# Moving work between VectorE and ScalarE around a branch: second half of batch 0's layernorm sums, sums of the weights, and the order of a few small steps

## The chip, the cores and the metric

The kernel runs on one core of a Trainium2 chip. The metric is the time of one execution on the device in microseconds (us), as the median of a few runs. A core has five engines that work side by side, each through its own list of instructions in order: TensorE (in the profile PE for matmuls, PEld for weight loads), VectorE (DVE), ScalarE (ACT), GpSimd (POOL) and SyncE (SP), which here only issues transfers. They wait for one another through semaphores. TensorE writes its results to PSUM, in banks of 128 x 512 numbers, and VectorE or ScalarE must take them from there before a bank can be used again.

## What is computed

Two graph layers over 32 batches of 512 x 512, all in float32. Each begins with a layernorm over the last axis and a maximum with 0. Layer 0 aggregates with `adj` and multiplies with a weight; layer 1 is attention with eight heads and a mask.

```python
# layer 0
h = jnp.maximum(_layernorm(x, axis=-1), 0.0)
x = x + einsum('bnd,do->bno', einsum('nm,bmd->bnd', adj, h), weight) + bias
# layer 1
h = jnp.maximum(_layernorm(x, axis=-1), 0.0)
q, k, v = h @ Wq + bq, h @ Wk + bk, h @ Wv + bv          # 8 heads of 64
scores = einsum('bqhd,bkhd->bhqk', q, k) / sqrt(64) + (1.0 - adj) * -1e9
x = x + einsum('bhqk,bkhd->bqhd', softmax(scores), v) @ Wo + bo
```

The mask subtracts (1 - adj) x 1e9. Where a row of `adj` has a largest entry that is ahead of the next by enough, the softmax puts the whole weight on that one place, and attention is a copy of the row of h that stands there. The kernel proves this from bounds at its start, and then computes layer 1 as h @ (Wv Wo) for the rows that are pointed at, and gathers the results. A general path exists for other inputs; it doesn't run here.

## The kernel before

A 512 x 512 matrix lies in SBUF as a tile of 128 partitions by four chunks of 512. Most products are made by `product()` (line 445): it splits each matrix in 2 x 2 blocks of 256 and forms the result from seven block products instead of eight, with sums of blocks prepared on VectorE. `sum_a` (line 324) makes the four sums of the left matrix, `sum_b` (line 336) those of the right, each one VectorE instruction over 128 x 512. The seven pieces come in the order p1, p5, u2, c11, c22, c12, c21. Three PSUM banks are added up over several pieces: p1, u2, c22 and c21 share one, so u2 can't begin before p1's value was taken out. A piece is taken by a `take`: in the product that forms yT (`take_new`) ScalarE copies p1, p5, u2 and c21 (line 490) and VectorE adds c11, c22 and c12 (line 488); in the product of layer 0 (`take_onto`) VectorE adds all seven onto x (line 508).

**Ahead of the branch** (lines 88 to 308) the order of the instructions is written out by hand. Wv and Wo are folded into wvo (`fold`, line 142, seven block products as above); adj is turned over on TensorE (`transposed`); batch 0 is normalised (`norms[0]`, `norms[1]`, two chunks each). `peaks(c)` (line 155) finds the eight largest entries of a chunk of adj's rows and marks where the first stands. `both` adds the four marks, TensorE counts them by columns (line 261), and `used` (line 279) says which rows of h are pointed at. TensorE counts these (line 264), VectorE decides (`decide`, line 243), TensorE spreads the decision (line 269), and `flag` (line 292) goes to every engine, which branch on it (lines 310 to 317). Beside this, layer 0's aggregate of batch 0 (line 270) runs on TensorE in four groups d = 0 to 3 of four products.

**Behind the branch** `single_path` (line 405) loops over the batches. For each, `todo` holds 21 lists of small steps, filled with `put(batch, step, function)`. They are handed out in three rows of seven: steps 0 to 6 go with the pieces of layer 0 of batch b, 7 to 13 with those of the aggregate of batch b + 1, and 14 to 20 with those of layer 1 of batch b - 1. In front of a piece's take, the functions of its step are issued (lines 477 to 480), so a step stands in each engine's list ahead of that take. For b = 0 the first row is `layer0_rows` (line 573) with only four steps, steps 4 to 6 are added to step 3, and the third row has no products: its steps are issued at once.

A layernorm comes in two kinds with the same interface. `Norm` (line 348) takes the sums of a row on VectorE (BATCH_NORM_STATS2, line 359, and an aggregate, line 360). `NormAct` (line 381) takes them on ScalarE, with two activations that add up along the row (line 389), each followed by a read of the accumulator. In both, `power()` makes 1 / sqrt(variance + eps) on GpSimd (lines 366 and 398), `offset()` makes the bias on VectorE, and `relu()` applies all on ScalarE (line 377). `halves` are the two halves of batch b's second layernorm, of layer 1, each over two of the four chunks.

Two queues matter for what follows. GpSimd scatters the rows of h to DRAM (`put_h`, line 582) with four indirect transfers in steps 9 and 11; SP loads them back in another order (`get_h`, line 597, step 16) and loads the next x.

Of the kernel before, what the change touches and what calls it, by code (L numbers as in the profile page):

```python
# [25 lines left out]
def gnn_two_layers(ctx: ExitStack, tc: tile.TileContext, x, adj, w0, b0, wq, bq, wk, bk, wv, bv, wo, bo, out):  # L26
# [15 lines left out]
    nc = tc.nc  # L42
# [10 lines left out]
    adjT, yT, w0_s, sel, wvo = big("adjT"), big("yT"), big("w0_s"), big("sel"), big("wvo")  # L53
# [18 lines left out]
    with ExitStack() as tmp, tc.manual_schedule():  # L72
# [82 lines left out]
        def peaks(c):  # L155
            nc.vector.max(top[:, c, :], adj_s[:, c, :])  # L156
            nc.vector.tensor_scalar(sel[:, c, :], adj_s[:, c, :], top[:, c, 0:1], None, op0=ALU.is_equal)  # L157
# [15 lines left out]
        u, v, w = (bank(i) for i in (0, 1, 2))  # L173
# [27 lines left out]
        flips = transposed(adj_s, adjT)  # L201
        next(flips)
        fold(u, wvT_t[:, 2], wo_t[:, 2], False)
        peaks(1)
        norms[1].offset()
        nc.vector.tensor_add(blk(wvo, 1, 1), u, blk(wvo, 1, 1))
        next(flips)
        next(flips)
        fold(v, wvT_t[:, 3], wo_blk(1, 1), False)
# [46 lines left out]
        for d in range(DC):  # L256
            ps = bank((2, 1, 0, 2)[d]).rearrange("p a n -> p (a n)")
            for m in range(C):
                if d == 1 and m == 2:
                    for i in range(C):  # L260
                        nc.tensor.matmul(few[:, 0, i:i + 1], both[:, i * P:(i + 1) * P], ones[:, 0:1],
                                         start=True, stop=True)
                if d == 2 and m == 1:
                    nc.tensor.matmul(many[:, 0, :], ones, used, start=True, stop=True)
                    nc.tensor.matmul(many[:, 1, :], ones, sums, start=True, stop=True)
                if d == 2 and m == 3:
                    nc.tensor.matmul(bias, ones, part, start=True, stop=True)
                if d == 3 and m == 1:
                    nc.tensor.matmul(few[0:1, 1, 0:1], sure, ones[:, 0:1], start=True, stop=True)
                nc.tensor.matmul(ps, hs[0][:, m, d * P:(d + 1) * P], adjT[:, m, :], start=(m == 0), stop=(m == C - 1))  # L270
            if d == 0:
                squares(0)
            nc.scalar.copy(yT[:, d, :], ps)
            if d == 0:
                squares(1)
                for i in range(4):
                    sum_b(nc, adjT_s, adjT, i)
            if d == 1:
                nc.vector.tensor_scalar_min(used, few[:, 0, :], 1.0)
                if B > 1:  # L280
                    norms.append(NormAct(nc, small, mhalf, xs[1], hs[1], range(C)))
                    for c in range(C):
                        norms[2].stats(c)
                for i in range(2):
                    sum_b(nc, w0_t, w0_s, i)
            if d == 2:
                decide()
                nc.vector.memset(before[:, 0:1], 0.0)
                for m in range(1, C + 1):
                    nc.vector.tensor_add(before[:, m:m + 1], before[:, m - 1:m], many[:, 0, m - 1:m])  # L290
                nc.vector.tensor_add(cvo, bias, cvo)
# [28 lines left out]
def blk(t, chunks, cols, half=256):  # L320
    return t[:, 2 * chunks:2 * chunks + 2, cols * half:(cols + 1) * half]
# [83 lines left out]
def single_path(ctx: ExitStack, tc: tile.TileContext, x, wv, bv, wo, bo, out, kept, room):  # L405
# [15 lines left out]
    nc = tc.nc  # L421
# [127 lines left out]
    def norm(src, dst, chunks, kind=Norm):  # L549
        return kind(nc, small, mhalf, src, dst, chunks)  # L550
# [152 lines left out]
    with tc.manual_schedule():  # L703
        nc.gpsimd.affine_select(out=upper, in_=ones, compare_op=ALU.is_ge, fill=0.0, base=-1,
                                pattern=[[1, P]], channel_multiplier=-1)
        for b in range(B + 1):
            todo = [[] for _ in range(21)]

            def put(batch, step, f, *args):
                if 0 <= batch < B:  # L710
                    todo[step].append(lambda: f(batch, *args))

            put(b - 2, 15 if b == B - 1 else 1, fetch if b > B - 2 else finish)
            if b < 2:
                put(b + 2, 2 * b, load_x)
            if b > 0:
                put(b + 3, 15, load_x)
            for i, step in enumerate((0, 1, 2, 3) if b != 1 else (1, 2, 3, 4)):
                put(b + 1, step, h0_sum, i)
            put(b - 2, 14 if b == B - 1 else 0, put_z, 0, 6)  # L720
            if b == B - 1:
                put(b - 2, 13, put_z, 6, S)
            for r, step in enumerate((10, 11, 12) if b in (1, B - 1) else (5, 7, 8) if b < B else ()):
                put(b - 1, step, transpose_h, r)
            for c, step in enumerate((1, 3, 9, 12) if b == 0 else (9, 10, 11, 12) if b == B - 2 else (14, 15, 17, 19)):
                put(b + 1, step, add_b0, c)
            if b < B:
                H1[b] = work.tile([P, C, D], F32, name="h1")
                halves = [norm(X[b], H1[b], [2 * i, 2 * i + 1], Norm if b > 0 else NormAct) for i in range(2)]
            put(b, 6 if b > 0 else 1, lambda b: halves[0].stats(0))  # L730
            put(b, 6 if b > 0 else 2, lambda b: halves[0].stats(1))
            put(b, 6 if b > 0 else 7, lambda b: halves[0].power())
            put(b, 7 if b > 0 else 3, lambda b: halves[1].stats(0))
            put(b, 7, lambda b: halves[0].offset())
            put(b, 10 if b == B - 1 else 8, lambda b: halves[0].relu(0, b < B - 1))
            put(b, 8 if b > 0 else 7, lambda b: halves[1].stats(1))
            put(b, 8 if b > 0 else 7, lambda b: halves[1].power())
            put(b, 10 if b == B - 1 else 9, lambda b: halves[0].relu(1, b < B - 1))
            put(b, 10 if b == B - 1 else 9, put_h, 0)
            put(b, 9, lambda b: halves[1].offset())  # L740
            put(b, 10, lambda b: halves[1].relu(0, b < B - 1))
            put(b, 10, lambda b: halves[1].relu(1, b < B - 1))
            put(b, 11, put_h, 2)
            if b < B - 1:
                put(b - 2, 12, store)
            if b < B - 1:
                put(b, 16, get_h)
            else:
                put(b, 13, get_all)
                for c in range(C):  # L750
                    put(b, 15 + c, add_cvo, c)
            for i, step in enumerate((12, 13, 13, 14) if b in (1, B - 1) else (11, 11, 12, 12) if b < B else ()):
                put(b - 1, step, hT_sum, i)
            for i, step in enumerate((13, 13, 13, 14) if b in (0, B - 2) else (14, 15, 16, 18)):
                put(b + 1, step, yT_sum, i)
            if b < B and b != B - 2:
                put(b - 1, 20, put_z, 6, S)
            ahead = []
            if b == 0:
                put(2, 1, lambda b: ahead.append(ln0(b, NormAct)))  # L760
                for c, step in enumerate((1, 1, 2, 2)):
                    put(2, step, lambda b, c: ahead[0].stats(c), c)
            else:
                put(b + 2, 8, lambda b: ahead.append(ln0(b)))
                for c, step in enumerate((9, 10, 13, 13)):
                    put(b + 2, step, lambda b, c: ahead[0].stats(c), c)
            put(b + 2, 14 if b > 0 else 11, lambda b: ahead[0].power())
            put(b + 2, 17 if b > 0 else 12, lambda b: ahead[0].offset())
            for c, step in enumerate((17, 18, 19, 20) if b > 0 else (12, 13, 14, 14)):
                put(b + 2, step, lambda b, c: ahead[0].relu(c), c)  # L770
            if b == 0:
                put(0, 1, lambda b: number_rows())
                for i in (2, 3):
                    put(0, 12, lambda b, i: sum_b(nc, w0_t, w0_s, i), i)
                    put(0, 13, lambda b, i: sum_a(nc, wvo_t, wvo, i), i)
                todo[3] += todo[4] + todo[5] + todo[6]
                run(layer0_rows(0), todo[0:4])
            if b == B - 1:
                put(b, 19, lambda b: transpose_all(0))
            if b == 1:  # L780
                tables = []
                put(1, 0, lambda b: tables.append(places()))
                put(1, 16, lambda b: look_up(tables[0]))
            if 0 < b < B:
                run(layer0(b), todo[0:7])
            elif b == B:
                run(None, todo[0:7])
            run(aggregate(b + 1) if b + 1 < B else layer1(b - 2) if b < B else None, todo[7:14])
            run(layer1(b - 1) if 0 < b < B and b != B - 2 else None, todo[14:21])
# [262 lines left out]
```

## Time and profile before

| | |
|---|---|
| median of 3 runs | 1081.98 us (1081.93 to 1082.1) |
| the profiled execution, its own time | 1081.54 us |
| its span in the trace | 1079.7 us |
| granted TensorE clock | 0.999 |
| VectorE busy / ScalarE busy / GpSimd busy | 898.7 / 376.2 / 447.1 us |
| flag written (VectorE, line 292) | at 37.05 us |
| first layer 0 product behind the branch (TensorE, line 577) | at 40.51 us |
| first aggregate product in the loop (TensorE, line 451) | at 54.77 us |
| first layer 0 product of batch 1 | at 67.98 us |

All times in the trace count from the start of the span. A line of the timeline gives the start, the busy time, the engine, the line of the kernel, the operation, what it writes and reads, and in brackets how long the engine was idle before it and what it waited for. Instructions on VectorE and ScalarE overlap a little: a sum of 128 x 512 on VectorE shows 0.68 us, and the next begins 0.60 us after its start. The waits are idle time in front of an instruction, put down to the instruction elsewhere that ended it.

### The profile page before, as it was taken

What the parts mean: (1) busy time and instruction counts of PE and PEld (TensorE: products, weight loads), DVE (VectorE), ACT (ScalarE), POOL (GpSimd) and SP (SyncE); (2) the same over time, 40 slices, a digit from 0 to 9 for tenths busy, and PEclk for the clock granted to TensorE, in tenths of its full rate; (3) what the DMA queues carried; (4) which work ended last, traced back from release to release, by engine and by line L of the source; (5) the groups of instructions that cost most, each with busy time, mean ns of one, the idle gap of its engine ahead of it and who ended that gap; (6) DMA issues with size and microseconds to landing.
All of it is one profiled execution on the core that took longest, in us unless ns stands there. A gap on an engine that the chain in (4) does not pass through costs nothing.

```text
span 1079.7 us, 16014 instructions
## 1 busy us (share of the span) xinstructions
PE 1066.3 (99%) x5448; PEld 946.2 (88%) x5448; DVE 898.7 (83%) x1837; ACT 376.2 (35%) x709; POOL 447.1 (41%) x522
## 2 busy tenths in 40 slices
PE   9999999999999999999999999999999999999996
PEld 7478989999998999988999988999998999998993
DVE  6868888888888888888888888888888888888874
ACT  4744323334422324322323432323432323432331
POOL 2024554343554343554343454443454434355413
PEclk9999999999999999999999999999999999999999
DMA  9154666657776666767666767666776666766538
GB/s 330 40 92 145 183 184 160 157 169 197 186 185 158 165 168 187 193 174 183 148 169 184 199 170 195 143 168 175 205 187 183 148 157 180 199 180 165 133 106 272
DMA packets 162700, 186.92 MB, mean 173 GB/s; under 512 B 15024, under 2 KB 102832, under 8 KB 162608
## 3 DMA queue, kind: packets, MB, share of 16 engines
q1 hardware_dynamic: 132592, 116.73, 36.8%
q0 software_dynamic: 27968, 66.61, 27.4%
q10 hardware_dynamic: 2048, 2.46, 0.7%
q8 instruction: 45, 0.74, 0.3%
q14 instruction: 47, 0.39, 0.1%
HBM read 96.28 MB, written 89.46 MB: 172 GB/s over the span
## 4 chain that ended last, share of the span: by engine, by line
PE 93%; DVE 3%; DMA 2%; issue 1%; POOL 1%; ACTq 0%; ACT 0%; POOLq 0%; DVEq 0%
PE mm L451 91%; PE mm L577 1%; DMA x<-in_L_gnn_Wv_dram 1%; PE mm L270 1%; DMA yT<-z,place 1%; DMA z<-hc 0%; POOL hs L589 0%; DVE top L156 0%; DVE part L163 0%; DVE hc L656 0%; DVE st L359 0%; POOL rstd L398 0%; DVE sel L157 0%; DVE both L223 0%; POOL yT L674 0%
## 5 line engine op out<-in xcount | busy, mean ns | idle before, releaser
L665 POOL DMA_INDIRECT x<-z,place x116 | 182.8, 1576 | 351.3 <-issue 194.3
L490 ACT COPY yT<-mm 128x512 f32<-128x512 f32 x124 | 71.9, 580 | 541.9 <-PE mm L451 538.8
L508 DVE TENSOR_TENSOR x<-mm,x 128x512 f32<-128x512 f32 x217 | 149.8, 690 | 86.9 <-PE mm L451 86.9
L377 ACT ACTIVATE h<-x,off,rstd 128x512 f32<-128x512 f32 x256 | 194.5, 807 | 39.9 <-DVE off L369 35.8
L366 POOL TENSOR_TENSOR rstd<-ve,mhalf 128x2 f32<-128x2 f32 (+1 forms) x93 | 102.5, 1102 | 200.0 <-DVE ve L365 200.0
L451 PE MATMUL mm<-w_t,sel 128*128 128x256 f32 x744 | 171.0, 379 | 1.2 <-DVE x L508 1.2
L451 PE MATMUL mm<-adjT_s,h0s 128*128 128x256 f32 x744 | 171.0, 379 | 0.9 <-ACT yT L490 0.9
L359 DVE BATCH_NORM_STATS2 st<-x 128x6 f32<-128x512 f32 x244 | 163.4, 670 | 1.1
L451 PEld LDWEIGHTS mm<-w_t,sel 128*128 128x128 f32 x744 | 141.2, 190 | 20.8 <-DVE x L508 1.6
L451 PEld LDWEIGHTS mm<-adjT_s,h0s 128*128 128x128 f32 x744 | 141.2, 190 | 20.6 <-ACT yT L490 1.5
L589 POOL DMA_INDIRECT hs<-h,dest x124 | 133.2, 1074 | 23.6 <-issue 22.4
L451 PE MATMUL mm<-w_s,yT 128*128 128x256 f32 x496 | 117.2, 379 | 0.0
L451 PE MATMUL mm<-adjT,h 128*128 128x256 f32 x496 | 117.2, 379 | 0.0
L451 PE MATMUL mm<-hTs,wvo_t 128*128 128x168 f32 x720 | 112.4, 306 | 0.0
L501 ACT ACTIVATE zs<-mm,cvo_c 128x168 f32<-128x168 f32 x240 | 83.1, 397 | 75.0 <-PE mm L451 75.0
L451 PEld LDWEIGHTS mm<-adjT,h 128*128 128x128 f32 x496 | 94.2, 190 | 13.2 <-ACT h L389 0.2
L451 PEld LDWEIGHTS mm<-hTs,wvo_t 128*128 128x128 f32 x720 | 105.5, 190 | 0.0
L451 PEld LDWEIGHTS mm<-w_s,yT 128*128 128x128 f32 x496 | 92.9, 190 | 11.3
L557 DVE TENSOR_TENSOR x<-x,b_r 128x512 f32<-128x512 f32 x124 | 84.0, 677 | 0.0
L451 PE MATMUL mm<-hT,wvo 128*128 128x168 f32 x480 | 78.2, 306 | 0.0
L451 PEld LDWEIGHTS mm<-hT,wvo 128*128 128x128 f32 x480 | 72.7, 190 | 1.6
L488 DVE TENSOR_TENSOR yT<-mm,yT 128x512 f32<-128x512 f32 x93 | 64.0, 688 | 9.4 <-PE mm L451 4.9
(181 smaller groups left out, 1313.3 us busy)
## 6 DMA issues: line engine op xcount, KB each, us to landing
out_dram<-x SPq DMA_DIRECT2D x124, 256.0 KB, 4.7
x<-in_x_dram SPq DMA_DIRECT2D x120, 256.0 KB, 4.9
hc<-hs SPq DMA_DIRECT2D x124, 176.0 KB, 3.1
z<-zr SPq DMA_DIRECT2D x120, 96.0 KB, 2.0
z<-zr SPq DMA_DIRECT2D x120, 80.0 KB, 1.9
hs<-h,dest POOLq DMA_INDIRECT x124, 6.0
x<-z,place POOLq DMA_INDIRECT x116, 5.8
adj_s<-in_adj_dram SPq DMA_DIRECT2D x2, 512.0 KB, 5.8
```

The lines of the kernel that those rows point to most:

```text
L270: nc.tensor.matmul(ps, hs[0][:, m, d * P:(d + 1) * P], adjT[:, m, :], start=(m == 0), stop=(m == C - 1))
L359: self.nc.vector.bn_stats(st, self.src[:, self.chunks[i], :])
L366: self.nc.gpsimd.tensor_tensor(self.rstd, ve, self.mhalf[:, 0:n], ALU.pow)
L377: self.nc.scalar.activation(dst, src, AF.Relu, bias=self.off[:, i:i + 1], scale=self.rstd[:, i:i + 1])
L451: nc.tensor.matmul(bank[:, m, 0:half], lhs[:, k, m * P:(m + 1) * P], rhs[:, k, :], start=(first and m == 0 and k == 0), stop=(k == 1), ski ...
L488: nc.vector.tensor_add(dst, bank, dst)
L490: nc.scalar.copy(dst, bank)
L501: nc.scalar.activation(dst[:, m, :], bank[:, m, :], AF.Identity, bias=cvo_c[:, 2 * i + m:2 * i + m + 1])
L508: nc.vector.tensor_add(dst, bank, dst)
L557: nc.vector.tensor_add(X[b][:, c, :], X[b][:, c, :], b0_r)
L589: stored = nc.gpsimd.indirect_dma_start(out=HS[b], out_offset=bass.IndirectOffsetOnAxis(ap=dest[:, i:i + 1], axis=0), in_=H1[b][:, i, :], ...
L665: nc.gpsimd.indirect_dma_start(out=X[b][:, c, :], out_offset=None, in_=Z[b], in_offset=bass.IndirectOffsetOnAxis(ap=place[:, c:c + 1], axi ...
```

## The change

Four things are moved; nothing is computed otherwise, apart from the way the sums of one half layernorm are formed.

1. Ahead of the branch, the addition of a fold product to wvo and the offset of the second half of batch 0's first layernorm stand ahead of `peaks(1)`. Before, the order was peaks, offset, addition.
2. The fourth sum of adjT stands behind `used` instead of ahead of it.
3. The second half (chunks 2 and 3) of batch 0's second layernorm is a `Norm` instead of a `NormAct`: its row sums are taken on VectorE.
4. The third and fourth sums of w0 go from step 12 to step 8, those of wvo from step 13 to step 9.

```diff
@@ -201,9 +201,9 @@
         flips = transposed(adj_s, adjT)
         next(flips)
         fold(u, wvT_t[:, 2], wo_t[:, 2], False)
+        nc.vector.tensor_add(blk(wvo, 1, 1), u, blk(wvo, 1, 1))
+        norms[1].offset()
         peaks(1)
-        norms[1].offset()
-        nc.vector.tensor_add(blk(wvo, 1, 1), u, blk(wvo, 1, 1))
         next(flips)
         next(flips)
         fold(v, wvT_t[:, 3], wo_blk(1, 1), False)
@@ -273,10 +273,11 @@
             nc.scalar.copy(yT[:, d, :], ps)
             if d == 0:
                 squares(1)
-                for i in range(4):
+                for i in range(3):
                     sum_b(nc, adjT_s, adjT, i)
             if d == 1:
                 nc.vector.tensor_scalar_min(used, few[:, 0, :], 1.0)
+                sum_b(nc, adjT_s, adjT, 3)
                 if B > 1:
                     norms.append(NormAct(nc, small, mhalf, xs[1], hs[1], range(C)))
                     for c in range(C):
@@ -726,7 +727,7 @@
             if b < B:
                 H1[b] = work.tile([P, C, D], F32, name="h1")
-                halves = [norm(X[b], H1[b], [2 * i, 2 * i + 1], Norm if b > 0 else NormAct) for i in range(2)]
+                halves = [norm(X[b], H1[b], [2 * i, 2 * i + 1], Norm if b > 0 or i == 1 else NormAct) for i in range(2)]
             put(b, 6 if b > 0 else 1, lambda b: halves[0].stats(0))
@@ -771,8 +772,8 @@
                 for i in (2, 3):
-                    put(0, 12, lambda b, i: sum_b(nc, w0_t, w0_s, i), i)
-                    put(0, 13, lambda b, i: sum_a(nc, wvo_t, wvo, i), i)
+                    put(0, 8, lambda b, i: sum_b(nc, w0_t, w0_s, i), i)
+                    put(0, 9, lambda b, i: sum_a(nc, wvo_t, wvo, i), i)
                 todo[3] += todo[4] + todo[5] + todo[6]
```

`halves[1].stats(0)` is issued in step 3 and `halves[1].stats(1)` and `power()` in step 7 of batch 0; these steps are the same before and after.

## The prediction

> **What bounds the kernel now.** First the page: shares of busy time, then the chain that ended last, by engine.
>
> ```profile
> PE 1066.3 (99%) x5448; PEld 946.2 (88%) x5448; DVE 898.7 (83%) x1837; ACT 376.2 (35%) x709; POOL 447.1 (41%) x522
> ...
> PE 93%; DVE 3%; DMA 2%; issue 1%; POOL 1%; ACTq 0%; ACT 0%; POOLq 0%; DVEq 0%
> ```
>
> TensorE is the bound, and a change that leaves its products alone can win only the time in which it stands still. So the second view is the waits of TensorE over the whole run (total, times, longest, in us; two lines, of the first and the last microseconds, left out):
>
> ```profile
> ...
> PE mm L451 <- DVE x L508: 1.2, 1, 1.2
> PE mm L451 <- ACT yT L490: 0.9, 1, 0.9
> ...
> PE mm L577 <- ACT yT L273: 0.7, 1, 0.7
> PE mm L149 <- DVE wvo L206: 0.4, 1, 0.4
> PE mm L451 <- DVE zs L498: 0.3, 1, 0.3
> PE few L264 <- DVE used L279: 0.2, 1, 0.2
> ```
>
> Each occurs once, and all lie in the first 101 us. Behind them the chain is TensorE's products without a wait up to 1054 us, so what is won early stays won. Third, the timeline of TensorE around the two largest (start, length):
>
> ```profile
> 54.77 1.89 PE L451 MATMUL mm<-adjT,h 128*128 128x256 f32 x8
> 56.49 1.89 PE L451 MATMUL mm<-adjT_s,h0s 128*128 128x256 f32 x8
> 59.24 1.99 PE L451 MATMUL mm<-adjT_s,h0s 128*128 128x256 f32 x8 [0.86 <-ACT yT L490]
> 61.07 1.89 PE L451 MATMUL mm<-adjT,h 128*128 128x256 f32 x8
> ...
> 69.70 1.89 PE L451 MATMUL mm<-w_t,sel 128*128 128x256 f32 x8
> 72.79 1.99 PE L451 MATMUL mm<-w_t,sel 128*128 128x256 f32 x8 [1.20 <-DVE x L508]
> 74.62 1.89 PE L451 MATMUL mm<-w_s,yT 128*128 128x256 f32 x8
> ```
>
> Undisturbed, a product starts 1.726 us after the one before (54.77 to 56.49, 61.07 to 69.70 is five such steps). Around the first wait two steps take 61.07 - 56.49 = 4.58 us, 1.13 more than 2 x 1.726; around the second 74.62 - 69.70 = 4.92 us, 1.47 more. A stall costs about 0.27 us more than the listed wait, because matmul ends in the list are modelled and the weights come late as well. I count in starts. Last, all engines where these waits end:
>
> ```profile
> 19.16 0.69 DVE L156 MAX8 top<-adj_s 128x8 f32<-128x512 f32 x1
> ...
> 20.28 0.15 DVE L369 SCALAR_TENSOR_TENSOR off<-mv,rstd 128x2 f32<-128x2 f32 x1
> 20.35 0.68 DVE L206 TENSOR_TENSOR wvo<-mm,wvo 128x512 f32<-128x512 f32 x1
> ...
> 21.09 1.99 PE L149 MATMUL mm<-wvo_t,yT 128*128 128x256 f32 x8 [0.36 <-DVE wvo L206]
> ...
> 31.68 0.15 DVE L279 TENSOR_SCALAR used<-few 128x4 f32<-128x4 f32 x1
> ...
> 31.89 0.39 PE L264 MATMUL few<-used,ones 128*128 128x4 f32 x2 [0.19 <-DVE used L279]
> ```
>
> ```profile
> 58.62 0.57 ACT L490 COPY yT<-mm 128x512 f32<-128x512 f32 x1
> ...
> 70.25 0.68 DVE L331 TENSOR_TENSOR wvo_t<-wvo 128x512 f32<-128x512 f32 x1
> ...
> 72.06 0.68 DVE L508 TENSOR_TENSOR x<-mm,x 128x512 f32<-128x512 f32 x1
> ```
>
> The copy at 58.62 frees the bank of a product that was done at 54.77 + 1.89 = 56.66: ScalarE was working off eight rounds of layernorm sums, back to back from 46.93 to 58.6. The addition at 72.06 takes a product done at 69.87, behind seven sums on VectorE.
>
> **What the Trainium skill says.** "GPSIMD Engine Reference", section 1 (Specifications): GpSimd shares its SBUF interfaces with VectorE, and is disturbed by VectorE instructions with two SBUF inputs. The trace agrees: the power of two columns takes 0.70 us at 82.72, beside x<-mm,x with one input in PSUM, but 1.07 at 59.00 beside x<-x,b_r. "Perfetto Trace Analysis", section "Tensor Engine Instruction": the end of a matmul in a trace is estimated, which is why I count starts; the 1.13 against 0.86 here agrees.
>
> **The change, part by part.**
>
> A. *L201-206.* The addition to wvo goes ahead of peaks(1). VectorE's cadence from starts: 0.60 a sum, 0.72 the maximum, 0.40 the comparison, 0.07 the offset. Before: 19.16 + 0.72 + 0.40 + 0.07 + 0.60 = 20.95, when peaks(2) begins. Now the addition starts at 19.16 (its product, 16.17 + 1.96 = 18.13, is done) and ends at 19.84. The last fold of TensorE then follows at 20.57 instead of 21.09, and layer 0's first product at 18.84 + 2 x 1.726 = 22.29 instead of 22.92: 0.63 earlier. But offset() now stands directly behind the addition and needs GpSimd's power (19.33 to 20.03; one input of the addition is in PSUM, so I take 0.70; at 1.07 all below is 0.37 later). It starts at 20.07, not 19.76. peaks(1) starts at 20.14, peaks(2) at 21.26: VectorE is 0.31 later, and has no gap up to `used`. That delays the chain that matters.
>
> B. *L276-281.* One sum of adjT behind `used` instead of ahead: 0.60 earlier. So `used` starts at 31.68 + 0.31 - 0.60 = 31.39, and TensorE's counts at 31.60 (0.21 behind, as before) instead of 31.89. TensorE would be ready at about 30.8, so most of the 0.63 is lost in a longer wait for `used`. Gain of A and B together: **0.29 us**. Bounds: 0 if the power is slowed, 0.5 if offset does not wait. The sum that is moved back is hidden: decide() ends about 34.5, and its product is not due before 36.5. ScalarE's squares end at 31.33, hidden too. The 0.72 us ahead of L577 (last copy of yT) stays, only shifted, and so do the flag and VectorE behind it.
>
> C. *L729, second half on VectorE.* ScalarE loses two rounds of 1.46 us (46.93, 48.41, 49.87...): it is free at 55.4 instead of 58.6. VectorE gains two BATCH_NORM_STATS2 (0.72 with gap) and two aggregates (0.18): 1.8 us. The first falls into its wait of 1.54 us ahead of 54.97, so it costs nothing; without that cover, 0.87. The second stands behind offset of the first half (56.26 after the shift) and ends about 57.3; `ve` follows, and GpSimd's power from 57.53, slowed by the sums of D to at most 1.41 (the highest in this trace). So the second half's rstd is there at 58.94 instead of 60.07. The first product, done at 56.37, is copied at 56.4 to 57.0, and the third starts at once at 57.93: the whole **1.13 us**.
>
> D. *L774-775, four sums.* They leave VectorE's run before 72.06 (4 x 0.60 = 2.4 us) and go to steps 8 and 9, about 57.5 to 60.9 with add_b0 and offset among them. VectorE was idle there for 2.03 us and, up to 63.07, for 0.60 + 2.80. Its next take, c11, is done by TensorE at 61.55: hidden. What is next late? GpSimd: four scatters of about 1.3 us each, first at 59.1 (was 60.25), the last ends about 64.1; the power behind them ends at 65.2; offset, 0.08; the c12 addition at 65.3 (product done at 65.0); three sums of yT to 67.9; the fourth needs ScalarE's c21 copy at 67.5; L508 about 68.5, as its product is done at 68.45. It ends at 69.2, and TensorE wants it at 69.8. Slack 0.6 us, so the whole **1.47 us**. SP's loads of hc, table and x[3] are only issued earlier, in the same order.
>
> After that everything moves with TensorE. The wait at L498 (about 100.8) stays. Sum: 0.29 + 1.13 + 1.47 = **2.89 us**. The profiled execution took 1081.54 us, 1079.7 of them span; it becomes 1078.65. The median is 0.44 above the profiled execution, so **1079.1 us**. No change can be told within 0.2%, 2.16 us: faster means below 1079.82.
>
> **Rivals.**
>
> 1. GpSimd replaces VectorE. If slowed scatters put the power more than 0.6 us later, offset at step 12 holds the c12 addition and the yT sums behind it, and the last stall returns. Against it is the slack; for it, that GpSimd now works beside two-input sums. All of D lost: 1081.98 - 1.42 = 1080.56; half lost, 1079.8.
> 2. The stalls are worth only what the list says: 0.86 + 1.20, and nothing from A and B because `used` comes no earlier: 1079.92. For it: the 0.31 us delay of VectorE eats half of B already. Against it: the starts.
> 3. Slower: VectorE becomes late in the loop. Batch 0's last layer-1 product waited for L498 at 100.89, worth 100.89 to 102.13 and before 2.82 - 2 x 1.14 = 0.54 us. If the new phase of the engines makes that return in each of some 29 batches, +15.7 - 2.9: 1094.8. It decides from 2.89 / 29 = 0.10 us a batch. Against it: VectorE still waits for TensorE at 88.7 and 90.4, so its lag is renewed from TensorE each batch, and the order from batch 1 on is untouched.
>
> **How the numbers follow.** Forecast 62%, its own range 1078.5 to 1079.8; rival 1 16%; rival 2 14%; rival 3 6%; a still larger gain (the wait at L498 gone as well: 1078.5) 2%. Range 1078.5 to 1080.6, which takes in rivals 1 and 2. Faster 0.64, same 0.30, slower 0.06.
>
> **What would show it.** The waits of TensorE for L490 and L508 gone, the one for L206 gone, the one for L279 grown to about 0.7 us; L264 at 31.6; aggregate's third product at 57.9; layer 0's at 70.0; two more L359 between 52 and 58. A wait for L508 or L488 left in 60 to 75, or a releaser POOL L398 ahead of it, makes rival 1 right; a wait for L498 in many batches, rival 3.

## The result, and the profile after

The changed kernel takes 1080.11 us, the kernel before 1082.1 (medians of nine runs each, on the same chip). The medians differ by 2.0 us. The ratio of the two kernels is put at 0.9978, with a 95% interval of 0.9970 to 0.9987: 2.4 us less, and between 1.4 and 3.2. The forecast was 1079.1 us, with a range of 1078.5 to 1080.6. The profiled execution took 1079.28 us, with a span of 1077.5 us, where that of before had 1079.7.

The page of the changed kernel: busy time by engine, and the chain that ended last by engine.

```profile
PE 1065.8 (99%) x5448; PEld 946.4 (88%) x5448; DVE 900.1 (84%) x1841; ACT 373.2 (35%) x701; POOL 447.2 (42%) x522
...
PE 95%; DVE 2%; DMA 1%; issue 0%; ACT 0%; POOL 0%; ACTq 0%; POOLq 0%; DVEq 0%
```

VectorE has four instructions more, ScalarE eight less, and TensorE's share of the chain went from 93 to 95%. (One line was added, so the lines of the kernel before from 280 on are one higher in this profile.) The waits of TensorE over the run (total, times, longest):

```profile
PE pt L169 <- POOL ident masks.py:199: 1.4, 1, 1.4
PE few L264 <- DVE used L279: 0.8, 1, 0.8
PE mm L628 <- issue: 0.8, 1, 0.8
PE mm L578 <- ACT yT L273: 0.7, 1, 0.7
PE mm L452 <- issue: 0.3, 1, 0.3
```

The 1.2 us for layer 0's addition, the 0.9 us for ScalarE's copy and the 0.4 us for the addition to wvo are gone. The wait for `used` grew from 0.2 to 0.8. The last line is the wait ahead of batch 0's last layer-1 product (now at 98.07), which was forecast to stay. In the timeline of TensorE the two pieces with a stall are now in one run of sixteen matmuls with the piece ahead of them:

```profile
56.27 3.62 PE L452 MATMUL mm<-adjT_s,h0s 128*128 128x256 f32 x16
59.72 1.89 PE L452 MATMUL mm<-adjT,h 128*128 128x256 f32 x8
...
68.36 3.62 PE L452 MATMUL mm<-w_t,sel 128*128 128x256 f32 x16
71.81 1.89 PE L452 MATMUL mm<-w_s,yT 128*128 128x256 f32 x8
```

From the first aggregate product (54.54, before 54.77) to 59.72 there are 5.18 us, before 6.30: 1.12 won. From there to 71.81 there are 12.09, before 13.55: 1.46 won. These are the two large terms of the forecast, 1.13 and 1.47. The third term didn't come. All engines ahead of the branch:

```profile
18.61 1.89 PE L149 MATMUL mm<-x,x 128*128 128x256 f32 x8
...
18.93 0.69 DVE L204 TENSOR_TENSOR wvo<-mm,wvo 128x512 f32<-128x512 f32 x1
...
19.84 0.16 DVE L370 SCALAR_TENSOR_TENSOR off<-mv,rstd 128x2 f32<-128x2 f32 x1 [0.21 <-POOL rstd L367]
...
21.52 0.78 POOL L198 DMA_DIRECT2D bt<-in_L_gnn_bk_dram  x1
21.76 0.79 DVE L157 TENSOR_SCALAR sel<-adj_s,top 128x512 f32<-128x512 f32 x1
...
31.46 0.15 DVE L279 TENSOR_SCALAR used<-few 128x4 f32<-128x4 f32 x1
...
31.67 0.38 PE L264 MATMUL few<-used,ones 128*128 128x4 f32 x2 [0.82 <-DVE used L279]
```

The first weights arrive at slightly different times in each execution, so this part is counted from the fold product at 18.61 (18.84 before), which stands ahead of every edit's effect. From there to the count at line 264 there are 13.06 us, before 13.05: nothing won. VectorE waits 0.21 us at the offset, as forecast, and then its comparison of peaks(2) takes 0.79 us instead of 0.49, beside a small transfer that GpSimd is issuing. In the trace of before the same comparison falls between the issues of two such transfers:

```profile
20.98 0.81 POOL L198 DMA_DIRECT2D bt<-in_L_gnn_bq_dram  x1
...
21.67 0.49 DVE L157 TENSOR_SCALAR sel<-adj_s,top 128x512 f32<-128x512 f32 x1
21.75 0.78 POOL L198 DMA_DIRECT2D bt<-in_L_gnn_bk_dram  x1
```

At 99.31 us TensorE begins batch 2's layer 0, 2.82 us ahead of before (102.13), of which 0.23 is the earlier start. At layer 1's last products, 1050.91 and 1053.25, it is 2.34 ahead. So the loop lost 0.48 us more than in the trace of before, without any line in the list of waits; the last section of the experiments deals with that.

### The profile page after: what moved, and what is told of

It is laid out like the page before. It is cut to its first block, busy times and chain, and to the rows that moved or that the text cites. A ratio compares the mean times of both kernels' runs of the same rounds, so it can differ in the third digit from the quotient of the medians.

```text
span 1077.5 us, 16010 instructions
## 1 busy us (share of the span) xinstructions
PE 1065.8 (99%) x5448; PEld 946.4 (88%) x5448; DVE 900.1 (84%) x1841; ACT 373.2 (35%) x701; POOL 447.2 (42%) x522
## 4 chain that ended last, share of the span: by engine, by line
PE 95%; DVE 2%; DMA 1%; issue 0%; ACT 0%; POOL 0%; ACTq 0%; POOLq 0%; DVEq 0%
PE mm L452 93%; PE mm L578 1%; DMA yT<-z,place 1%; PE mm L270 1%; PE pt L169 0%; DMA z<-hc 0%; DVE top L156 0%; DVE part L163 0%; DVE sel L157 0%; PE mm L149 0%; DVE x L680 0%; DVE st L360 0%; POOL rstd L367 0%; DVE both L223 0%; ACTq L662 0%
```

## The experiments

The effects are below what most medians tell apart, so the verdicts rest on starts in the traces: "count" is the distance from the fold product named above to TensorE's count at line 264, 13.05 us before. Where a kernel was timed in several runs, its ratio to before is given.

### Each edit behind the branch alone

Only the second half of the layernorm on VectorE:

```diff
-                halves = [norm(X[b], H1[b], [2 * i, 2 * i + 1], Norm if b > 0 else NormAct) for i in range(2)]
+                halves = [norm(X[b], H1[b], [2 * i, 2 * i + 1], Norm if b > 0 or i == 1 else NormAct) for i in range(2)]
```

> Only the second half of batch 0's second layernorm goes to VectorE; all else is as before. My theory (each of the two large stalls is removed by its own edit): the wait of TensorE for ScalarE's copy at aggregate's third product is gone, worth 1.13 us in starts; the wait for VectorE at layer 0's third product stays at about 1.2 us, since the seven sums still stand before it. Time: 1.1 us less than before. Rival (freeing ScalarE is enough for both, since everything behind it comes earlier): both waits gone, 2.6 us less. Rival (nothing is won, since VectorE now is late by the two rounds of sums): the stall comes back as a wait for VectorE in the aggregate, 0 to 0.3 us less.

The ratio is 0.9986 (0.9978 to 0.9994). The waits of TensorE:

```profile
PE mm L451 <- DVE x L508: 1.1, 1, 1.1
PE mm L577 <- ACT yT L273: 0.7, 1, 0.7
```

The wait for the copy at line 490 is gone from the list, the one for the addition at line 508 is there. From 54.39 to 59.57 TensorE took 5.18 us (before 6.30), and the second stretch, 59.57 to 73.06, took 13.49 (13.55). The edit removes its own stall, 1.12 us, and hardly touches the other. Both rivals fall.

Only the four sums:

```diff
-put(0, 12, lambda b, i: sum_b(nc, w0_t, w0_s, i), i)
-put(0, 13, lambda b, i: sum_a(nc, wvo_t, wvo, i), i)
+put(0, 8, lambda b, i: sum_b(nc, w0_t, w0_s, i), i)
+put(0, 9, lambda b, i: sum_a(nc, wvo_t, wvo, i), i)
```

> Only the four sums of w0 and wvo go to steps 8 and 9; all else is as before. My theory: the wait for VectorE at layer 0's third product is gone, worth 1.47 us in starts, and the wait of 0.86 us for ScalarE at aggregate's third product stays as it was. Time: 1.5 us less than before. Rival (the sums only move the wait: they delay a take in the aggregate, or GpSimd's power beside them): less than 0.8 us is won and a new wait shows between 60 and 70 us. Rival (the loop takes it back): the stalls are gone by 75 us, but less than 0.8 us arrives at the end.

The ratio is 0.9983 (0.9975 to 0.9991). The stretch from aggregate's fourth product, 60.97, to layer 0's fourth, 73.06, took 12.09 us: the whole 1.46. The stall for ScalarE stayed (0.89 listed). But in the profiled execution a wait of 1.28 us stood at layer 1's last product. All engines there:

```profile
95.42 3.22 POOL L366 TENSOR_TENSOR rstd<-ve,mhalf 128x4 f32<-128x4 f32 x1 [5.77 <-DVE ve L365]
...
97.05 0.68 DVE L557 TENSOR_TENSOR x<-x,b_r 128x512 f32<-128x512 f32 x1
...
98.67 0.16 DVE L369 SCALAR_TENSOR_TENSOR off<-mv,rstd 128x4 f32<-128x4 f32 x1 [0.94 <-POOL rstd L366]
...
100.33 0.84 PE L451 MATMUL mm<-hTs,wvo 128*128 128x168 f32 x4 [1.28 <-DVE zs L498]
```

GpSimd's power took 3.22 us, 1.41 in the trace of before. VectorE waited for it with the takes of layer 1 behind it, and so did TensorE. It gave back 1.0 of the 1.46 us. A second trace of the same kernel tells whether the edit does that:

> The four sums alone once more, for a second trace. In the first one GpSimd's power of batch 3's rows at 95.4 us took 3.22 us, where it takes 1.41 in every other trace; VectorE ran sums of two SBUF inputs back to back beside it, waited 0.94 us for it at the offset, and TensorE 1.28 us at layer 1's last product instead of 0.27, which gave back 1.0 of the 1.45 us won. If that is chance: 1.41 here, a wait of about 0.27, and a gain of 1.4 us that stays. If it is the price of moving the sums alone: 3.2 us again and a wait of 1.3 us.

```profile
95.60 1.41 POOL L366 TENSOR_TENSOR rstd<-ve,mhalf 128x4 f32<-128x4 f32 x1 [5.78 <-DVE ve L365]
```

Here the power took its usual time, the wait was 0.27 us, and TensorE reached batch 2's layer 0 at 100.74, 81.83 us behind the fold product; before it was 83.29. The 1.46 us stay. The long power doesn't belong to this edit: of the 14 traces of this study it stands in four, all of different kernels, two of them with nothing changed behind the branch. What brings it on is open.

Both together, with the order ahead of the branch as it was:

> The two edits behind the branch together, and the order ahead of the branch as before. My theory: 2.6 us are won by 75 us in starts of TensorE, as much as the sum of the two alone, and as much as the whole change has shown (its trace is 2.8 us ahead at 99 us, of which 0.2 us stood already at 18 us, before any changed instruction): so the part ahead of the branch gave nothing. At the end 2.0 to 2.6 us less, for the loop's rare stalls behind GpSimd's gathers can take some. Rival (the order ahead of the branch is worth its predicted 0.3 us): this one is 0.3 us slower than the whole change, by TensorE's starts as measured from its last fold product but one.

The ratio is 0.9979 (0.9969 to 0.9989). From the fold product to layer 0's fourth product there are 53.17 us; before 55.78, and in the changed kernel 53.20. So these two edits make the whole gain, 2.61 us, and it is the sum of the two alone (1.12 and 1.46) to within 0.03 us.

### The whole change again

> The whole change again, for a second trace. My theory: by 99 us TensorE is 2.6 to 2.9 us ahead of before, the same as in the first trace; between 100 and 1050 us a few stalls of 0.1 to 0.5 us appear in batches where the first gather onto x waits more than about 12.2 us for the z rows, in about the same batches as in the first trace (near 430, 461, 526, 623 us), but not the same lengths, so that 0 to 0.8 us is lost on the way. Rival (the loss of 0.5 us in the loop is a steady price of the change): the same batches stall by the same lengths to 0.05 us. For the comparison of peaks(2), which took 0.79 us in the first trace and 0.49 before: if it is the GpSimd transfer issued beside it, it is 0.79 here too; if chance, 0.49.

The ratio is 0.9978 (0.9968 to 0.9988). The count is 13.05 us, the comparison of peaks(2) takes 0.80 us, and layer 0's fourth product stands 53.19 us behind the fold product. So the slow comparison isn't chance, and the part ahead of the branch wins nothing in either trace. The stalls in the loop were not the same: batches stalled behind gathers at 461, 526 and 623 us, and the one at 429 lost only 0.10 us this time, where it had lost 0.48.

### The order ahead of the branch, taken apart

Only the addition and the offset ahead of peaks(1), as in the change:

> Only the addition and the offset go ahead of peaks(1); all else is as before. My theory: TensorE's last fold product comes 0.5 us earlier, but used comes 0.31 us later by the wait at the offset, and 0.3 us more by the slowed comparison: TensorE's count L264 0.6 us later than in before, counted from the start of the last fold product but one, so this edit alone makes the kernel slower. Prediction's own step: 0.31 us later. Rival (an earlier product is a gain): 0 to 0.5 us earlier.

```profile
32.31 0.39 PE L264 MATMUL few<-used,ones 128*128 128x4 f32 x2 [1.42 <-DVE used L279]
```

The fold product stands at 18.66, so the count is 13.65 us: 0.60 later than before. Alone this edit makes the start of the kernel slower, twice as much as the forecast's step said. TensorE comes earlier to a place where it must then wait 1.42 us.

Only the sum of adjT behind `used`:

```diff
-                for i in range(4):
+                for i in range(3):
                     sum_b(nc, adjT_s, adjT, i)
...
                 nc.vector.tensor_scalar_min(used, few[:, 0, :], 1.0)
+                sum_b(nc, adjT_s, adjT, 3)
```

> Only the fourth sum of adjT goes behind used; all else is as before. My theory: used starts 0.60 us earlier, TensorE's wait there (0.19 us listed) goes and its counts come when its own products are done: about 0.45 us earlier, counted from the start of the last fold product but one. The two large stalls and the rest stay. Rival (nothing is won there even so): less than 0.1 us earlier.

`used` came 0.6 us earlier, TensorE's wait for it is gone, and the count is 12.71 us: 0.34 won, 0.1 less than I expected. The two edits ahead of the branch are +0.60 and -0.34 alone; together they are 0 and not +0.26. Alone, the second lets `used` come 0.60 us earlier, but TensorE's own products leave room for 0.34 of it; behind the first, where TensorE waits for `used` in any case, all 0.60 count.

If the loss lies in the offset's wait and in what follows it, the offset can stand behind the peaks (the kernel offset_late):

```diff
         nc.vector.tensor_add(blk(wvo, 1, 1), u, blk(wvo, 1, 1))
-        norms[1].offset()
         peaks(1)
+        norms[1].offset()
```

> The whole change, but ahead of the branch the order is addition, peaks, offset: the addition is still early, and VectorE no longer meets GpSimd's power at the offset. My theory (the part ahead of the branch gave nothing because VectorE stood 0.2 to 0.3 us at the offset and its next comparison was then 0.3 us longer, which ate what moving the sum of adjT won): the offset follows without a wait, VectorE reaches peaks(2) when it did before, used comes 0.6 us earlier than in the whole change, counted from the start of the last fold product but one, and TensorE's count L264 too; 0.6 us faster than the whole change, 3.2 us (0.30%) faster than before. Rival (TensorE isn't held by used there, its wait is only made up from ScalarE's squares, which the count of the sums needs): L264 or L265 doesn't come earlier by more than 0.2 us.

```profile
20.05 0.71 DVE L157 TENSOR_SCALAR sel<-adj_s,top 128x512 f32<-128x512 f32 x1
...
21.31 0.94 POOL L198 DMA_DIRECT2D bt<-in_L_gnn_bk_dram  x1
21.46 0.49 DVE L157 TENSOR_SCALAR sel<-adj_s,top 128x512 f32<-128x512 f32 x1
...
30.87 0.16 DVE L279 TENSOR_SCALAR used<-few 128x4 f32<-128x4 f32 x1
...
31.08 0.39 PE L264 MATMUL few<-used,ones 128*128 128x4 f32 x2 [0.44 <-DVE used L279]
```

With the fold product at 18.40 the count is 12.68 us: 0.38 better than the change, not 0.6. The wait is gone, but now the comparison of peaks(1) is the slow one, 0.71 us, and it again lies beside one of GpSimd's transfers (19.55 to 20.54). The comparison of peaks(2) took 0.49 us beside the next transfer but one, whose issue began 0.15 us ahead of it; there it was the issue that was longer, 0.94 us instead of 0.78. The rival falls too, since more than 0.2 us was won. The ratio is 0.9977 (0.9968 to 0.9985), which can't be told from the change's.

So the transfers were taken from GpSimd (the kernel quiet_pool, otherwise the whole change): the three small ones go to SP's queue behind the first x, the two for the biases behind the second.

```diff
+        for t, d in ((bv_c, bv), (bt[0], bq), (bt[1], bk)):
+            nc.sync.dma_start(t, d.rearrange("(c p) -> p c", p=P))
...
+        for d, r in ((b0, b0_r), (bo, cvo)):
+            nc.sync.dma_start(r, bass.AP(tensor=d.tensor, offset=d.offset, ap=[[0, P], [1, D]]))
...
-        for t, d in ((bv_c, bv), (bt[0], bq), (bt[1], bk)):
-            nc.gpsimd.dma_start(t, d.rearrange("(c p) -> p c", p=P))
-        for d, r in ((b0, b0_r), (bo, cvo)):
-            nc.gpsimd.dma_start(r, bass.AP(tensor=d.tensor, offset=d.offset, ap=[[0, P], [1, D]]))
```

> The whole change, and the five small transfers that GpSimd issues beside the peaks are issued by SP instead, three of them behind the load of the first x, two behind that of the second. My theory (the comparison of peaks(2) took 0.8 us instead of 0.49 because a transfer was being issued on GpSimd, whose SBUF interface it shares): all four comparisons take 0.49 us, and L264 comes 0.3 us earlier than in the whole change, 12.75 us from the start of the last fold product but one instead of 13.05. Rival (the 0.8 us come from where the instruction stands, not from GpSimd): 0.8 again, and 13.05.

```profile
21.67 0.49 DVE L161 TENSOR_SCALAR sel<-adj_s,top 128x512 f32<-128x512 f32 x1
...
31.29 0.38 PE L264 MATMUL few<-used,ones 128*128 128x4 f32 x2 [0.53 <-DVE used L279]
```

All four comparisons take 0.49 us, and with the fold product at 18.52 the count is 12.77 us, 0.28 us less than in the change. So GpSimd's transfers were the cause of the slow comparison. It is their issue that disturbs and not their landing: in the trace of before they land at 26.2 us and later.

With the transfers on SP and the offset behind peaks(1), both delays should go (the kernel quiet_offset):

> As quiet_pool, and with the offset behind peaks(1). My theory: neither the wait at the offset nor a slowed comparison is left, L264 comes 0.6 us earlier than in the whole change (12.4 us from the start of the last fold product but one), TensorE's wait there is nearly gone, and the kernel is the fastest of all, 3.2 us faster than before by its trace up to 100 us. Rival (the transfers on SP come too late or hold up the weights): a wait for b0, for the sums of squares or for bv, and no gain.

```profile
31.20 0.39 PE L264 MATMUL few<-used,ones 128*128 128x4 f32 x2 [0.21 <-DVE used L279]
```

The fold product is at 18.75, so the count is 12.45 us, and TensorE begins batch 2's layer 0 at 98.84: 80.09 us behind the fold product, against 80.70 in the change and 83.29 before. By the trace this version is 0.6 us ahead of the change, and 3.2 of before. Its time is 1079.78 us, ratio 0.9975 (0.9967 to 0.9983): faster than before, but its interval and the change's overlap, so that it beats the change is shown for the first 100 us and not for the time.

### The loop

In the change's first trace 0.48 us more was lost between 100 and 1050 us than in the first trace of before. TensorE's starts there are regular but in a few batches. One of them, all engines:

```profile
434.85 1.54 POOL L666 DMA_INDIRECT x<-z,place  x1 [0.30 <-issue]
...
435.83 1.32 POOL L367 TENSOR_TENSOR rstd<-ve,mhalf 128x2 f32<-128x2 f32 x1
...
437.19 0.16 DVE L370 SCALAR_TENSOR_TENSOR off<-mv,rstd 128x2 f32<-128x2 f32 x1 [1.14 <-POOL rstd L367]
...
437.43 0.81 ACT L378 ACTIVATE h<-x,off,rstd 128x512 f32<-128x512 f32 x1 [1.99 <-DVE off L370]
...
438.15 0.56 ACT L491 COPY yT<-mm 128x512 f32<-128x512 f32 x1
...
439.33 0.57 ACT L491 COPY yT<-mm 128x512 f32<-128x512 f32 x1
...
439.95 1.59 PEld L452 LDWEIGHTS mm<-adjT_s,h0s 128*128 128x128 f32 x8 [0.35 <-ACT yT L491]
```

Read it downwards: the last of four gathers of z rows onto x; behind it in GpSimd's list the power of the layernorm; VectorE waits for that 1.14 us; ScalarE's activation waits 1.99 us for the offset, and ahead of the copies it delays them; TensorE's next piece needs the second copy. The first gather of this batch waited 12.78 us for the rows of z to land; in batches without a stall it mostly waits 11.0 to 11.6. If this costs the change something, the kernel before must show less of it:

> The kernel before once more, for a second trace. If the stalls in the loop are chance and no price of the change, they lie here between 0.5 and 1.4 us in all, as in the traces of the changed kernels (1.0 us twice, 0.8, 0.9); if the change makes them worse, at 0.5 us as in the first trace of before. The waits up to 101 us are as in the first trace.

Summed over all products that start more than 0.06 us behind the regular step, the loop loses 1.40 us here, and 0.70 in the first trace of before; 1.12 and 1.16 in the two traces of the change; 0.93 with the two edits behind the branch; 0.74 in the second trace of the sums. The same few batches come up, near 430, 461, 526 and 623 us. So this is scatter between executions, and no price of the change that these traces show.

An attempt to take it away moved the fourth gather behind the scatters, on top of offset_late:

```diff
-            put(b - 2, 15 if b == B - 1 else 1, fetch if b > B - 2 else finish)
...
+                put(b - 2, 1, finish, 0, 3)
...
             put(b, 11, put_h, 2)
+                put(b - 2, 11, finish, 3, C)
```

> As offset_late, and in the loop the last of the four gathers onto x is issued behind the scatters of the same batch (step 11) instead of with the other three (step 1). My theory (the rare stalls of 0.2 to 0.5 us in the loop come from GpSimd: where the z rows land late, the fourth gather pushes the power of the layernorm, then ScalarE's activation and copy, past TensorE): the power stands ready at its due time in every batch and no stall of TensorE is left between 100 and 1000 us; 0.3 to 0.6 us faster than offset_late. Rival (the stalls come from elsewhere, for example late x): the same batches stall. Rival (the later gather holds back the stores of x, and what SP has queued behind them): new waits of TensorE for the transposed h, slower than offset_late by more than 1 us.

The ratio is 1.0005 (0.9997 to 1.0014): all that the change won is lost. The last rival was right about the loss. SP's queue in one batch, first of offset_late and then of this kernel, gather_split (start, length, what is issued):

```profile
433.56 6.92 SPq L685 DMA_DIRECT2D out_dram<-x  x4
```

```profile
434.95 14.61 SPq L685 DMA_DIRECT2D out_dram<-x  x4
```

The stores of x wait for the fourth gather and take SP 14.61 us instead of 6.92; the load of x, the load of hc and the stores of z stand behind them. So the next gathers begin later: their wait is mostly 12.5 to 15.1 us instead of 11 to 13, and the stalls of the loop add up to 3.73 us in eight batches, 1.75 in four for offset_late. The expectation of no stall is refuted, but the cause that it named is borne out by a count of when a batch stalls. Take the distance from TensorE's first product of layer 0 in a batch to the start of that batch's first gather. In the 13 traces with four gathers in a row, no batch between 110 and 1000 us has a stall, counted as above, where it is 7.89 us or less, and every batch does from 7.92 us on. With three in a row here, none stalls up to 9.69 us, and every one does from 9.87 on. One gather less in front of the power lets the rows land 1.8 to 2.0 us later without a stall, and from one gather to the next there are 1.84 to 1.95 us. So the stalls come from the gathers ahead of the power in GpSimd's list; this kernel moved that limit, and moved the gathers by more.

## Why the prediction was right, point by point

**The time alone says little.** 1080.11 us lies outside the forecast's own range, 1078.5 to 1079.8, and within the whole range only because that takes in rivals 1 and 2; rival 2's figure, 1079.92, is nearer to it than 1079.1. Nor is it below 1079.82, which the forecast gave a chance of 0.64. What decides between the forecast and its rivals are the starts.

**The bound, and where time could be won.** TensorE's waits were the right place to look, and counting in starts was right: the two stalls, listed with 0.86 and 1.20 us, gave 1.12 and 1.46 when they went. Rival 2, which counted the listed waits, is refuted by both single edits.

**C, the second half on VectorE.** Forecast 1.13, measured 1.12 in both traces of it alone and together. The copy came as soon as its product was done, and the first half of the new work on VectorE lay in its wait (the idle time ahead of the addition at 54.74 fell from 1.54 to 0.72 us).

**D, the four sums.** Forecast 1.47, measured 1.46. Eight sums, not seven, stood ahead of line 508's addition in the trace of before (from 66.39 on, with one take among them). Rival 1 came closer than I had worked out. GpSimd's first scatter, beside the moved sums, took 1.42 us, not 1.09, but it also began at 58.85, ahead of the 59.1 of the forecast, so the power began at 64.15, as worked out. The power for four columns took 1.49 us, not 1.05. So the offset stood at 65.67 us instead of 65.2, and line 508's addition (509 in this profile) ended at 69.69 and not 69.2. TensorE wanted it at about 69.9: of the 0.6 us of slack, 0.2 was left.

**A and B, the order ahead of the branch: this is the step that failed.** The forecast put the two together at a gain of 0.29 us, as 0.60 from the sum that is moved back less 0.31 at the offset. The 0.60 and the 0.31 were there. Missing was 0.30 us on VectorE, the comparison of peaks(2) slowed by GpSimd's transfer, so that the term is 0.0. The sentence "and has no gap up to `used`" was true, but it took the durations of that row as fixed while moving the row against another engine's work. The bound of 0 that I gave for it came from another cause, a slowed power, which did not occur: it took 0.70 us. That the term lay at its bound is luck. The upper bound, 0.5 us, was too low: without the wait and without the slow comparison 0.60 us were won (13.05 less 12.45, in quiet_offset). And one sign of the forecast came true by luck: TensorE's count stood at 31.67 us, forecast at 31.6, only because this execution was 0.23 us early at the fold product already.

**What is won early stays won.** Nearly. The list of waits shows no wait in the loop, yet the kernel before loses 0.7 to 1.4 us there, in stalls too short or too hidden for the list. The waits for L498 in many batches, rival 3, did not come; a loop that stalls now and then was already there, at GpSimd's gathers.

**The sum.** 2.89 forecast; 2.59 by TensorE's starts at batch 2 (83.29 less 80.70); 2.4 by the ratio, with an interval of 1.4 to 3.2, and 2.0 between the medians. Of the 0.30 us between the forecast and the starts, 0.29 is the term of A and B. Between the starts at 100 us and the end the loop adds a scatter of up to 0.7 us between two traces of the same kernel (0.70 and 1.40), so these runs don't fix the sum any closer.

## What to carry to other kernels

Where one engine is the bound, price a stall from the starts of its instructions against their regular step, not from the listed wait, and take each stall with the edit that removes its releaser: here these gains added up, 1.12 and 1.46 us to 2.61. When a row of instructions is moved by a few tenths of a microsecond, look at what the other engines are doing at its new place: here GpSimd's issue of a transfer took back the 0.3 us that the move was to win. And before work is moved past a transfer's release, follow what stands behind it in the queue that issues the next transfers.

## What the runs showed of the hardware

- VectorE's comparison of 128 x 512 with a column took 0.49 us, and 0.79 or 0.80 when it began 0.24 us after GpSimd had begun to issue the transfer of bv, bq or bk, 0.71 or 0.69 when it began 0.50 us after. With the transfers issued by SP it took 0.49 at the same place. Begun 0.11 us ahead of such an issue (before, at 19.88), or 0.69 us after its begin (at 21.67), it took 0.49 too. It also took 0.49 when it began 0.15 us after (offset_late, at 21.46), where the issue took 0.94 us instead of 0.78; and 0.36 us into the issue of the transfer of bo (before, at 23.40). The Trainium skill, "GPSIMD Engine Reference", section 1, says that GpSimd's SBUF interfaces are shared with VectorE and names the 2-port mode as one case of contention, and "VectorE: DVE Perf Modes", section "Mode 2×_2P", counts this form of instruction in that mode for float32. The traces agree that the two disturb each other, and show it both ways: VectorE longer by up to 0.31 us in five of them, GpSimd by 0.16 us in two. What decides which one is held is not shown.
- The same power on GpSimd took 3.21 or 3.22 us instead of 1.41 in four of 14 traces, always at the same place, beside four VectorE additions in a row with two SBUF inputs. In the case shown it ended 0.9 us after the last of these. Why it does so in some executions and not in others stayed open.
- A copy of z onto x (a gather) took GpSimd 1.53 to 1.65 us to issue, and the next in the row began 1.84 to 1.95 us after its start. Why z lands late in the same few batches of most traces stayed open.
